# Turning some edge counts behind a layer's experts, making masks tile by tile, and starting a row product between the turns

## The chip, the cores and the metric

The kernel runs on one core of a Trainium2 chip. A core has a matrix engine (TensorE, PE in the profile, whose weight loads are listed as PEld), three engines for elementwise work (VectorE or DVE, ScalarE or ACT, GpSimd or POOL), queues that start transfers (SP among them) and 16 DMA engines. The metric is the device time of one execution in microseconds (us). Three runs of the kernel before took 1514.17 to 1518.64 us, with a median of 1517.61.

## The reference

The program is a chain of four layers on 625 nodes with 512 features and 10,000 directed edges. Each layer is a graph part and an expert part, and each part adds its result to x after a layer normalisation of its input:

```
edge_index = jnp.stack([src, dst])
x = x + _L0_gnn_ref(_layernorm(x, axis=-1), edge_index, ...)
x = x + _L0_ffn_ref(_layernorm(x, axis=-1)[None], ...)[0]
x = x + _L1_gnn_ref(_layernorm(x, axis=-1), edge_index, ...)
...
x = x + _L3_gnn_ref(_layernorm(x, axis=-1), edge_index, ...)
x = x + _L3_ffn_ref(_layernorm(x, axis=-1)[None], ...)[0]
```

Three of these parts meet the change. The expert part of layer L0 has eight small experts, each of which is computed for every node and weighted by a gate:

```
hid = jax.nn.gelu(jnp.einsum('bnd,edf->bnef', y, W1) + b1)
eo = jnp.einsum('bnef,efd->bned', hid, W2) + b2
out = jnp.einsum('bned,bne->bnd', eo, gate)
```

The graph part of layer L1 is an attention over the edges, twice. For each edge a score of its two ends is taken, the scores of a target's edges go through a softmax, and the values of the sources are summed with these weights:

```
scores = jnp.einsum('ehd,ehd->eh', q[tgt], k[srcidx])
m = jax.ops.segment_max(scores, tgt, num_segments=n)
p = jnp.exp(scores - m[tgt])
s = jax.ops.segment_sum(p, tgt, num_segments=n)
w = p / (s[tgt] + 1e-16)
agg = jax.ops.segment_sum(w[:, :, None] * v[srcidx], tgt, num_segments=n)
```

The graph part of layer L3 multiplies the rows by a matrix, sums them over the edges with a loop at each node, and normalises over the nodes:

```
xw = x @ W.T
...
msgs = norm[:, None] * xw[row]
out = jax.ops.segment_sum(msgs, col, num_segments=n)
```

## The kernel before

The 625 nodes lie in five tiles of 125 (`NT`, `T`), the 512 features in four blocks of 128 (`KD`). x stays on the chip with nodes on the partitions. Products need the features on the partitions, so each normalised tile is turned: `to_features` (L400) takes, per tile, four transposes on PE (L408) into one bank of PSUM and copies it out by `evac` (L267 on DVE, L275 on ACT, by turns). All uses of PSUM share one pool of four buffers that go round.

The edges are held as a matrix of counts, `aT`, source by target: the setup builds it by products of one-hot columns. The attention of L1 treats the graph as a dense matrix: for each target tile it computes all 625 scores, adds a mask of -1e30 where the count is zero (L1263), takes the exponential (L1268) and multiplies by the count (L1278). For this it needs the counts with targets on the partitions, `cnt`, and the mask of the same shape. `cnt` is made in front of the experts of L0: for each of five tiles, five transposes of blocks of `aT` (L1609) and two copies, one of 500 columns and one of 125. The mask is one instruction on POOL over all five tiles (L1618).

`small_experts` (L1201) runs the eight experts three ahead: `Hidden.half` (L1191) gives an expert's hidden units, `add` (L1211, L1213) its second product and the weighted sum into x on DVE. A bias of the experts is prepared by small copies on POOL and comes in by products (L634, L641). The last three experts go tile by tile, and behind each tile `ln.add` takes its statistics: for tiles 0 and 2 by two passes on ACT (L343, L344), for the others by DVE (L335, L350). The normalisation `LayerNorm` closes in two groups, tiles 0 to 2 and tiles 3 and 4: a square root on ACT (L296), some small steps on DVE (L300 to L309), and then the tiles themselves by turns on DVE (L371) and ACT (L377), the latter after `ln_nb` (L374). At its end `small_experts` issues two products whose result nobody reads (`warm`, L398).

In L1 the query projection goes through `mm_groups` (L466): it takes all four PSUM buffers at once and its results are copied by four instructions on DVE (L1669). The key projection (L477) and its copies follow, and then the first scores (L1257). Five additions of a bias row to x (L1688) are queued behind the last query copy.

In L3 the normalised rows are turned first, all five tiles, and then `mm_nodes` (L485) multiplies them tile by tile by the weights, with the results copied by DVE and ACT by turns (L1901); the product with `aT` follows (L477). The profile lists two passes for one such product of float32: a tile's row product of four steps is eight passes.

The order of instructions on each engine is not that of the source: a scheduler sets it when the program is built, from the data dependencies and the order of the source, and `tc.issue_after(i)` keeps what it encloses behind the instruction i on its engine. An example that matters here: the addition of the identity to the diagonal blocks of `aT` (named `loop` in `normalise`, L1646), written in the second half of L1, stands on DVE directly behind the count turns, since each waits only for the turn that reads its block. Weights come in chunks of 1 MB into three buffers, asked for by `take` on SP's queue.

Of the kernel before, what the change touches and what calls it, by code (L numbers as in the profile page):

```python
# [13 lines left out]
BF16 = mybir.dt.bfloat16  # L14
I32 = mybir.dt.int32
AF = mybir.ActivationFunctionType
OP = mybir.AluOpType
# [3 lines left out]
N = 625  # L21
NT = 5
T = N // NT
HC = 313
NP = 2 * HC
# [8 lines left out]
NEG = -1.0e30  # L34
# [161 lines left out]
def kernel(  # L196
# [11 lines left out]
    nc = tc.nc  # L208
# [20 lines left out]
    ident = const.tile([P, P], F32, name="ident")  # L229
# [82 lines left out]
    GROUPS = ((0, 3), (3, NT))  # L312
# [73 lines left out]
    def pstile(name):  # L386
        return psum.tile([P, 2, 512], F32, tag="ps", name=name)

    pe = {}

    def warm(n, behind=True):

        if n == 0:
            return
        with tc.issue_after(pe["last"].ins) if behind else nullcontext():
            ps = pstile("ps_warm")
            for _ in range(n):
                nc.tensor.matmul(ps[:, 0, :HC], ident, rows[:, :HC], start=True, stop=True)  # L398

    def to_features(src, name, scale=None, bias=None):  # L400

        dst = ttile(name)
        nc.gpsimd.memset(dst[:, :, N:NP], 0.0)
        if bias is None:
            for t in range(NT):
                ps = pstile("ps_tr")
                for k in range(KD):
                    pe["last"] = nc.tensor.transpose(ps[:, 0, k * T:(k + 1) * T],  # L408
                                                     src[:, t, k * P:(k + 1) * P], ident[:T, :T])
                evac(dst[:, :, t * T:(t + 1) * T],  # L410
                     ps[:, 0, :KD * T].rearrange("p (k t) -> p k t", t=T), scale)
        else:
            for k in range(KD):
                ps = pstile("ps_tr")
                for t in range(NT):
                    nc.tensor.transpose(ps[:, t // 4, (t % 4) * T:(t % 4 + 1) * T],
                                        src[:, t, k * P:(k + 1) * P], ident[:T, :T])
                s, b = scale[:, k:k + 1], bias[:, k:k + 1]
                evac(dst[:, k, :4 * T], ps[:, 0, :4 * T], s, b)
                evac(dst[:, k, 4 * T:N], ps[:, 1, :T], s, b)  # L420
        return dst
# [776 lines left out]
                if e == E - 1:  # L1198
                    table_of(AF.Sqrt, done)

    def small_experts(hidden, comb, layer, ln):  # L1201

        hs, ws = hidden.hs, hidden.ws

        def ahead(e):
            hidden.half(e, 0)
            hidden.half(e, 1)

        def add(e, t):
            ps = pstile("ps_eo")  # L1210
            pe["last"] = nc.tensor.matmul(ps[:T, 0, :], hs[e][:, t * T:(t + 1) * T],  # L1211
                                          ws[e // 4][1][:, e % 4, :], start=True, stop=True)
            nc.vector.scalar_tensor_tensor(x[:, t, :], ps[:T, 0, :], comb[:, t, e:e + 1],  # L1213
                                           x[:, t, :], op0=OP.mult, op1=OP.add)

        bias = expert_bias(comb, layer)
        bias.pop(0)()
        for e in range(len(hs), 3):
            ahead(e)
        for e in range(E - 3):  # L1220
            ahead(e + 3)
            for step in bias[3 * e - 3:3 * e] if e else ():
                step()
            for t in range(NT):
                add(e, t)

        for t in range(NT):
            for e in range(E - 3, E):
                add(e, t)
            ln.add(t, x[:, t, :], t in (0, 2))  # L1230
        warm(2)

    def attention(qT, kT, v, mask, counts, pt_pool, s_pool, values=lambda: None):

# [136 lines left out]
    aT = aT1[:T]  # L1371
    dg = const.tile([P, NP], F32, name="dg")
    xn = ktile("xn")
    hT = ttile("hT")
    with tc.tile_pool(name="setup", bufs=1) as setup, \
# [11 lines left out]
        for src in srcs:  # L1387
# [7 lines left out]
                                       op0=OP.mult, op1=OP.add)  # L1395
        nc.vector.tensor_scalar(digit[:, 1, :], digit[:, 0, :], float(BASE - 1), 1.0, op0=OP.mult,
                                op1=OP.add)
# [204 lines left out]
    with tc.tile_pool(name="l1g", bufs=1) as pool:  # L1602

        cnt = pool.tile([T, NT, NP], F32, name="cnt")
        nc.gpsimd.memset(cnt[:, :, N:NP], 0.0)
        for t in range(NT):
            ps = pstile("ps_ct")
            for j in range(NT):
                nc.tensor.transpose(ps[:T, j // 4, (j % 4) * T:(j % 4 + 1) * T],  # L1609
                                    aT[:, j, t * T:(t + 1) * T], ident[:T, :T])  # L1610
            evac(cnt[:, t, :4 * T], ps[:T, 0, :4 * T])
            evac(cnt[:, t, 4 * T:N], ps[:T, 1, :T])
        xn = ktile("xn")
        with tc.tile_pool(name="l0h", bufs=4) as hpool:
            small_experts(Hidden(yT, vec("L0_ffn_b1"), hpool), gate, 0,
                          LayerNorm(xn, groups=GROUPS))
        mask = pool.tile([T, NT, NP], BF16, name="mask")
        nc.gpsimd.tensor_scalar(mask, cnt, 0.0, NEG, op0=OP.is_equal, op1=OP.mult)  # L1618

# [32 lines left out]
        def step(n):  # L1654
            for work in steps[:n]:
                work()
            del steps[:n]

        xT = to_features(xn, "xT")
        for l in range(2):  # L1660
            if l == 1:
                normalise()
            with tc.tile_pool(name=f"l1p{l}", bufs=2) as pt_pool, \
                    tc.tile_pool(name=f"l1s{l}", bufs=4) as s_pool:
                (w,) = take(1)
                qT = ttile("qT")
                for o, ps in enumerate(mm_groups(
                        ONE, KD, lambda o, k: w[:, k, o * P:(o + 1) * P], xT)):
                    last = nc.vector.tensor_scalar(halves(qT[:, o, :]), ps,  # L1669
                                                   vec("L1_gnn_bq", l)[:, o:o + 1], DH ** -0.5,  # L1670
                                                   op0=OP.add, op1=OP.mult)
                    step(2)
                (w,) = take(1)
                kT = ttile("kT")
                for o in range(KD):
                    ps = mm_features([(w[:, k, o * P:(o + 1) * P], xT[:, k, :]) for k in range(KD)])
                    evac(halves(kT[:, o, :]), ps)
                    step(2)
                (w,) = take(1)
                v = ktile("v")  # L1680

                def values():
                    for t in range(NT):
                        evac(v[:, t, :], mm_nodes(xT, w, t))
                        step(2)
                        if l == 0:
                            with tc.issue_after(last.ins):
                                nc.vector.tensor_add(x[:, t, :], x[:, t, :], row("L1_gnn_ln_b"))  # L1688

                oT = attention(qT, kT, v, mask, cnt, pt_pool, s_pool, values)  # L1690
                assert not steps
            (w,) = take(1)
            hT = ttile("hT")
            bn = BatchNorm(hT, THREE, vec("L1_gnn_g1", l), vec("L1_gnn_beta1", l), AF.Identity)
            for o in range(KD):
                ps = mm_features([(w[:, k, o * P:(o + 1) * P], oT[:, k, :]) for k in range(KD)])
                with bn.behind():
                    nc.vector.scalar_tensor_tensor(halves(hT[:, o, :]), ps,
                                                   vec("L1_gnn_bo", l)[:, o:o + 1],
                                                   halves(xT[:, o, :]), op0=OP.add, op1=OP.add)  # L1700
                    bn.add(o)
            (w,) = take(1)
            wf = w.rearrange("p k m -> p (k m)")
            (ps,) = mm_groups(THREE, 1, lambda o, k: wf[:, k * P:(k + 1) * P], hT)
            f = pool.tile([P, NP], F32, name="f", tag="f")
            nc.scalar.activation(halves(f), ps, AF.Relu, bias=vec("L1_gnn_b1", l))
            xT = ttile("xT")
            bn = BatchNorm(xT, TWO if l else ONE, vec("L1_gnn_g2", l), vec("L1_gnn_beta2", l),
                           AF.Identity)
            for o in range(KD):  # L1710
                ps = mm_features([(wf[:, D + o * P:D + (o + 1) * P], f)])
                with bn.behind():
                    nc.vector.scalar_tensor_tensor(halves(xT[:, o, :]), ps,
                                                   vec("L1_gnn_b2", l)[:, o:o + 1],
                                                   halves(hT[:, o, :]), op0=OP.add, op1=OP.add)
                    bn.add(o)
            warm(2)
# [175 lines left out]
        small_experts(hidden, comb, 2, LayerNorm(xn, groups=GROUPS))  # L1893


    xnT = to_features(xn, "xnT")
    (w,) = take(1)
    xw = ktile("xw")
    for t in range(NT):
        ps = mm_nodes(xnT, w, t)  # L1900
        last = nc.scalar.copy(xw[:, t, :], ps) if t % 2 else nc.vector.tensor_copy(xw[:, t, :], ps)  # L1901
    with tc.issue_after(last.ins):
        for t in range(NT):
            nc.vector.tensor_add(x[:, t, :], x[:, t, :], xn[:, t, :])
# [54 lines left out]
```

## Time and profile before

| | before |
|---|---|
| median of three runs | 1517.61 us (1514.17 to 1518.64) |
| profiled execution | 1512.58 us, span 1510.9 us |
| PE busy | 1434.1 us, 95% |
| DVE, ACT, POOL busy | 664.5, 389.0, 200.2 us |
| mean granted clock of PE | 0.985 |
| instructions | 18457 |

A timeline line gives the start, the time from the first start to the last end, the engine, the source line, the operation with its output and input, the shape, and how many were merged; in brackets stands how long the engine was idle before, and whose end let it go on. The granted clock is the share of PE's full speed that was allowed in a stretch. All times of single places are from the profiled execution.

### The profile page before, as it was taken

The page shows a single profiled execution, that of the slowest core. Times are in us where ns is not written, and L with a number is a line of the kernel's source. Part 1 is how long each engine was busy: PE and PEld are TensorE (multiplying, and loading weights), DVE is VectorE, ACT ScalarE, POOL GpSimd, SP SyncE. Part 2 cuts the span into 40 slices and gives each one's busy share as a digit, 9 for nine tenths or more (in the row PEclk, how much of TensorE's full clock was granted, in tenths as well). Part 3 has the DMA queues.
Part 4 walks back from the last instruction along what each step waited for, and adds up shares of the span by engine and source line. Part 5 has one row for each costly group of instructions (what it writes and reads, how often), then busy time and mean ns, then how long its engine had stood idle before and what let it go on. Part 6 is the DMA issues. An engine that isn't in the chain of part 4 may idle for free. (4 is left out here: it accounts for less than half of the span.)

```text
span 1510.9 us, 18457 instructions
## 1 busy us (share of the span) xinstructions
PE 1434.1 (95%) x7048; PEld 1002.9 (66%) x7048; DVE 664.5 (44%) x1793; ACT 389.0 (26%) x768; POOL 200.2 (13%) x344
## 2 busy tenths in 40 slices
PE   9999999999999999997999998999989999999996
PEld 6775466656565665565665886554667669999885
DVE  9945463363876546847512125746361101111100
ACT  2133273211466124633101105412130000001000
POOL 1010041300143013310202210000001001101000
PEclk9999999999999999998999999999999999999998
DMA  4010100111100110001768523000059326457880
GB/s 153 6 43 29 56 28 5 52 56 56 56 1 1 56 56 0 1 1 34 317 229 324 157 60 131 28 28 28 0 183 402 141 81 201 163 183 265 312 290 5
DMA packets 28915, 159.39 MB, mean 105 GB/s; under 512 B 3952, under 2 KB 4080, under 8 KB 11921
## 3 DMA queue, kind: packets, MB, share of 16 engines
q1 hardware_dynamic: 20791, 141.56, 25.5%
q0 software_dynamic: 5280, 11.27, 3.5%
q10 hardware_dynamic: 2746, 5.25, 1.1%
q8 instruction: 60, 0.98, 0.3%
q14 instruction: 38, 0.31, 0.1%
HBM read 166.49 MB, written 11.31 MB: 118 GB/s over the span
## 5 line engine op out<-in xcount | busy, mean ns | idle before, releaser
L955 PE MATMUL ps_h<-xgT,ring 128*128 128x128 f32 (+5 forms) x1920 | 318.6, 326 | 0.1
L955 PEld LDWEIGHTS ps_h<-xgT,ring 128*128 128x128 f32 x1920 | 276.5, 191 | 38.9 <-issue 3.5
L1286 POOL TENSOR_SCALAR s<-s,rs 125x625 f32<-125x625 f32 (+4 forms) x120 | 96.3, 820 | 307.5 <-DVE rs L1283 284.8
L1045 PE MATMUL ps_y<-hT,ring 128*128 128x352 f32 (+4 forms) x640 | 137.0, 373 | 0.0
L1045 PEld LDWEIGHTS ps_y<-hT,ring 128*128 128x128 f32 x640 | 108.7, 190 | 24.3 <-issue 0.2
L1925 DVE TENSOR_TENSOR hT<-ps_h,g 128x512 f32<-128x512 f32 (+4 forms) x60 | 27.8, 464 | 198.5 <-ACT g L1924 192.1
L1268 ACT ACTIVATE s<-s,mn 125x626 f32<-125x626 f32 (+4 forms) x120 | 87.2, 743 | 61.0 <-DVE mn L1263 61.0
L1263 DVE CUSTOM_DVE_ANT_0 s<-ps_s,mask 125x626 f32<-125x626 f32 (+4 forms) x120 | 82.2, 718 | 30.9 <-PE ps_s L1257 29.9
L1924 ACT ACTIVATE g<-ps_h 128x512 f32<-128x512 f32 (+4 forms) x60 | 25.0, 416 | 250.8 <-PE ps_h L955 250.8
L1257 PE MATMUL ps_s<-kT,qT 64*125 64x313 f32 (+4 forms) x416 | 84.3, 454 | 5.1 <-DVE mn L1263 5.1
L915 POOL DMA_INDIRECT slots<-rows_hbm,node x26 | 25.5, 981 | 357.0 <-PE ps_x L933 190.3
L1278 DVE SCALAR_TENSOR_TENSOR s<-s,cnt 125x626 f32<-125x626 f32 x80 | 66.4, 849 | 12.2 <-ACT s L1268 12.1
L1300 PEld LDWEIGHTS ps_p<-ident,s 125*125 125x125 f32 x432 | 52.4, 190 | 28.6 <-issue 15.0
L1211 PE MATMUL ps_eo<-w,h 128*125 128x512 f32 x160 | 70.5, 593 | 0.6 <-ACT h L1196 0.6
L1321 PE MATMUL ps_o<-pT,v 125*64 125x375 f32 (+2 forms) x448 | 60.1, 413 | 9.1 <-DVE mn L1263 4.6
L1300 PE MATMUL ps_p<-ident,s 125*125 125x125 f32 x432 | 63.2, 288 | 4.2 <-DVE mn L1263 1.7
L1257 PEld LDWEIGHTS ps_s<-kT,qT 64*125 64x125 f32 x416 | 43.7, 184 | 32.3 <-DVE mn L1263 12.0
L1078 PE MATMUL ps_y<-ring,hT 128*128 128x512 f32 x128 | 56.9, 593 | 0.0
L1424 PE MATMUL ps_a<-dst,src 125*128 125x313 f16 x400 | 55.0, 297 | 1.3 <-DVE dst L1410 0.9
L1211 PEld LDWEIGHTS ps_eo<-w,h 128*125 128x125 f32 x160 | 29.8, 187 | 36.4 <-issue 30.7
L485 PE MATMUL ps_mn<-w,hxT 128*125 128x512 f32 x120 | 52.0, 593 | 0.6 <-ACT hxT L277 0.6
L267 DVE COPY yT<-ps_y 128x352 f32<-128x352 f32 (+4 forms) x17 | 7.2, 425 | 102.4 <-PE ps_y L1045 102.4
(424 smaller groups left out, 2016.1 us busy)
## 6 DMA issues: line engine op xcount, KB each, us to landing
ring<-in_weights SPq DMA_DIRECT2D x122, 1024.0 KB
w<-in_weights SPq DMA_DIRECT2D x27, 1024.0 KB
rows_hbm<-xn ACTq DMA_DIRECT2D x2, 1120.0 KB
x<-in_x SPq DMA_DIRECT2D x1, 1120.0 KB
sums<-x ACTq DMA_DIRECT2D x1, 1120.0 KB
x<-sums SPq DMA_DIRECT2D x5, 224.0 KB
out<-x ACTq DMA_DIRECT2D x1, 1120.0 KB
rows<-in_rows SPq DMA_DIRECT2D x1, 1052.0 KB
```

The lines of the kernel that those rows point to most:

```text
L955: pe["last"] = nc.tensor.matmul(ps[:, m, g * n:(g + 1) * n], w[:, k, j * P:(j + 1) * P], xgT[:, k, :n], start=(k == 0), stop=(k == KD - 1))
L1045: nc.tensor.matmul(ps[:, 0, :n], second(i, f)[:, d * P:(d + 1) * P], hT[:, f, :n], start=(f == 0), stop=(f == nf - 1))
L1078: nc.tensor.matmul(ps[:, 0, :], hT[:, f, m * B:m * B + rows], second(i, f), start=(f == 0), stop=(f == nf - 1))
L1211: pe["last"] = nc.tensor.matmul(ps[:T, 0, :], hs[e][:, t * T:(t + 1) * T], ws[e // 4][1][:, e % 4, :], start=True, stop=True)
L1257: nc.tensor.matmul(ps[hh][:T, i, :w], qT[rr, b, t * T:(t + 1) * T], kT[rr, b, i * w:(i + 1) * w], start=True, stop=True)
L1263: nc.vector.tensor_tensor_reduce(s[:, hh, :nb * w].rearrange("p (a c) -> p a c", a=nb), ps[hh][:T, :nb, :w], mask[:, t, :nb * w].rearrange ...
L1268: nc.scalar.activation(s[:, hh, :nb * w], s[:, hh, :nb * w], AF.Exp, bias=mn[:, hh:hh + 1], scale=-1.0, accum_out=sm[:, hh:hh + 1] if caus ...
L1278: nc.vector.scalar_tensor_tensor(s[:, hh, :], s[:, hh, :], 1.0, counts[:, t, :], op0=OP.mult, op1=OP.mult, accum_out=sm[:, hh:hh + 1])
L1286: nc.gpsimd.tensor_scalar(s[:, hh, :w], s[:, hh, :w], rs[:, hh:hh + 1], 1.0, op0=OP.mult, op1=OP.mult)
L1300: nc.tensor.transpose(pp[:T, hh, j * T:(j + 1) * T], s[:, hh, j * T:(j + 1) * T], ident[:T, :T])
L1321: nc.tensor.matmul(po[rr, 0, o:n * T], v[:, j, h * DH:(h + 1) * DH], pT[:, hh, j, o:n * T], start=(j == 0), stop=(j == nk - 1))
L1424: nc.tensor.matmul(pa[b // 2][:, b % 2, :HC], srcs[c % SRCS][:, b, :], dsts[c][:, :HC], start=(c == c0), stop=(c == c1 - 1))
```

## The change

The turning of the counts is put into a function of the tile, `turned`. Tiles 0 and 1 are turned where all five were, and each of these two is masked on POOL right away. Tiles 2 to 4 are turned by `others`, which `small_experts` calls in place of its two warm products, with all copies on ACT. Their masks are made on DVE, each behind one of the last three query copies of L1's first attention. In L3, `to_features` calls a function between the turns of tile 2 and tile 3, and this does the first tile's row product.

```diff
-    def to_features(src, name, scale=None, bias=None):
+    def to_features(src, name, scale=None, bias=None, between=None):
...
             for t in range(NT):
+                if t == 3 and between is not None:
+                    between(dst)
                 ps = pstile("ps_tr")
...
-    def small_experts(hidden, comb, layer, ln):
+    def small_experts(hidden, comb, layer, ln, fill=lambda: warm(2)):
...
-        warm(2)
+        fill()
...
-        for t in range(NT):
+        mask = pool.tile([T, NT, NP], BF16, name="mask")
+
+        def turned(t, copies):
             ps = pstile("ps_ct")
             for j in range(NT):
-                nc.tensor.transpose(ps[:T, j // 4, (j % 4) * T:(j % 4 + 1) * T],
-                                    aT[:, j, t * T:(t + 1) * T], ident[:T, :T])
-            evac(cnt[:, t, :4 * T], ps[:T, 0, :4 * T])
-            evac(cnt[:, t, 4 * T:N], ps[:T, 1, :T])
+                pe["last"] = nc.tensor.transpose(ps[:T, j // 4, (j % 4) * T:(j % 4 + 1) * T],
+                                                 aT[:, j, t * T:(t + 1) * T], ident[:T, :T])
+            copies[0](cnt[:, t, :4 * T], ps[:T, 0, :4 * T])
+            copies[1](cnt[:, t, 4 * T:N], ps[:T, 1, :T])
+
+        def masked(engine, t):
+            engine.tensor_scalar(mask[:, t, :], cnt[:, t, :], 0.0, NEG, op0=OP.is_equal,
+                                 op1=OP.mult)
+
+        def others():
+
+            for t in range(2, NT):
+                with tc.issue_after(pe["last"].ins):
+                    turned(t, (nc.scalar.copy, nc.scalar.copy))
+
+        for t in range(2):
+            turned(t, (evac, evac))
+            masked(nc.gpsimd, t)
         xn = ktile("xn")
         with tc.tile_pool(name="l0h", bufs=4) as hpool:
             small_experts(Hidden(yT, vec("L0_ffn_b1"), hpool), gate, 0,
-                          LayerNorm(xn, groups=GROUPS))
-        mask = pool.tile([T, NT, NP], BF16, name="mask")
-        nc.gpsimd.tensor_scalar(mask, cnt, 0.0, NEG, op0=OP.is_equal, op1=OP.mult)
+                          LayerNorm(xn, groups=GROUPS), others)
...
                                                    op0=OP.add, op1=OP.mult)
+                    if l == 0 and o > 0:
+                        with tc.issue_after(last.ins):
+                            masked(nc.vector, o + 1)
                     step(2)
...
-    xnT = to_features(xn, "xnT")
     (w,) = take(1)
     xw = ktile("xw")
-    for t in range(NT):
+
+    def weighted_rows(xnT, t):
         ps = mm_nodes(xnT, w, t)
-        last = nc.scalar.copy(xw[:, t, :], ps) if t % 2 else nc.vector.tensor_copy(xw[:, t, :], ps)
+        return nc.scalar.copy(xw[:, t, :], ps) if t % 2 else nc.vector.tensor_copy(xw[:, t, :], ps)
+
+    xnT = to_features(xn, "xnT", between=lambda dst: weighted_rows(dst, 0))
+    for t in range(1, NT):
+        last = weighted_rows(xnT, t)
```

## The prediction

> **What bounds the kernel now.** I read the busy shares first, then the chain that ended last, then the two places that the change touches as timelines, last the granted clock of their stretches.
>
> ```profile
> PE 1434.1 (95%) x7048; PEld 1002.9 (66%) x7048; DVE 664.5 (44%) x1793; ACT 389.0 (26%) x768; POOL 200.2 (13%) x344
> ...
> PE 34%; issue 2%; DVE 2%; ACT 1%; DMA 1%; POOL 0%; ACTq 0%; POOLq 0%; DVEq 0%
> ```
>
> TensorE (PE) is busy 95% of the span and leads the chain. So a pass taken off PE's unbroken stretches shortens the run; one put into a hole of PE costs nothing.
>
> The first place, layer L0's experts. PE before them:
>
> ```profile
> 266.98 2.56 PE L1609 MATMUL ps_ct<-ident,aT 125*125 125x125 f32 x22
> 269.38 17.03 PE L1191 MATMUL ps_mf<-yT,w 128*128 128x313 f32 x64
> ```
>
> The count turns stand directly ahead of the experts with no hole between them: 2.56/22 = 0.116 us each on the path. Behind the experts, where x is normalised and turned:
>
> ```profile
> 340.68 1.22 PE L398 MATMUL ps_warm<-rows,ident 128*128 128x313 f32 x4
> ...
> 342.94 0.65 PE L408 MATMUL ps_tr<-ident,xn 125*128 125x125 f32 x4 [1.04 <-DVE xn L371]
> 342.99 0.81 ACT L377 ACTIVATE xn<-x,ln_nb,ln_r 125x512 f32<-125x512 f32 x1 [4.07 <-DVE ln_nb L374]
> ...
> 346.52 0.65 PE L408 MATMUL ps_tr<-ident,xn 125*128 125x125 f32 x4 [1.59 <-DVE xn L371]
> ```
>
> PE waits here 1.04 us for the first normalised tile and 1.59 us for the second group (tiles 3, 4). ACT has been idle 4.07 us before its tile.
>
> The second place, the start of layer L3, has the same shape, and then its row products:
>
> ```profile
> 1047.48 0.65 PE L408 MATMUL ps_tr<-ident,xn 125*128 125x125 f32 x4 [1.05 <-DVE xn L371]
> 1048.40 1.07 PE L408 MATMUL ps_tr<-ident,xn 125*128 125x125 f32 x8 [0.27 <-ACT xn L377]
> 1051.49 2.01 PE L408 MATMUL ps_tr<-ident,xn 125*128 125x125 f32 x8 [2.02 <-DVE xn L371]
> 1053.30 19.38 PE L485 MATMUL ps_mn<-w,xnT 128*125 128x512 f32 x40
> ```
>
> The hole is 2.02 us, and the 40 passes behind it take 19.38 us. Why so long, the clock column tells (stretch, length, busy time of PE, PEld, DVE, ACT, POOL, clock, DMA share, GB/s):
>
> ```profile
> 1049.50:1051.50 2.00, 0.01 (x1) 0.01 (x1) 1.85 (x7) 0.35 (x2) 0.00 (x0) 0.77 0.00 0
> 1051.50:1053.30 1.80, 1.80 (x9) 1.59 (x10) 0.00 (x1) 1.39 (x2) 0.00 (x0) 0.50 0.00 0
> 1053.30:1057.30 4.00, 4.00 (x6) 1.65 (x6) 0.68 (x1) 0.00 (x0) 0.00 (x0) 0.50 0.01 4
> 1057.30:1064.00 6.70, 6.70 (x17) 2.89 (x16) 0.69 (x1) 0.59 (x1) 0.00 (x0) 0.99 0.00 0
> ```
>
> 0.77 over 2 us means half clock from about 1050.6; it lasts to about 1057.4, 6.8 us. Weight loads of these passes stand 0.428 us apart at full clock, 0.855 us at half.
>
> **The change, part by part.** All against the profiled execution: 1512.58 us, span 1510.9.
>
> (a) Fifteen of the 25 count turns leave the stretch before the experts: 15 x 0.116 = -1.75 us. The built order of PE puts the experts' first product straight behind the ten that stay. Its chunk was asked for long before, and DMA is at 0 while it runs, so no load takes the place of the turns. Three of the five additions of the identity to aT (L1646) move away with their turns.
>
> (b) The fifteen turns stand where two warm products stood, behind the last expert. Four passes of 1.22 us go, 15 x 0.116 = 1.75 us come, from 340.7 to 342.4 on the old time axis. The next turn waits for its tile until 342.94, so PE pays nothing. What may pay is the normalisation. ACT now copies six pieces of PSUM in its idle 4.07 us: the 500-wide ones follow each other at 0.45 to 0.56 us, the 125-wide take 0.27. From 341.4 that is ct2 to 342.1, ct3 to 342.8, the wide part of ct4 to 343.2; then comes tile 1's normalisation (before 342.99): +0.2 us, and +0.65 if each copy costs its full duration (3 x 0.56 + 2 x 0.28 from 341.4). The sixth copy stands before the first xT copy and the second group's square root on ACT: +0.3 there. On VectorE (DVE) three additions of 0.28 us stand in the second group's chain; two fall into its waits, and that chain has waited for ACT and the turns at 344.5 anyhow. I take +0.25 for the second group, from 0 to +0.85 (all three additions in full).
>
> (c) The masks. On POOL one instruction of 10.84 us (five tiles, 2.17 each) becomes two of a tile each, 4.3 us, ahead of the expert bias's pieces, which ended at 272.9 and would end near 277; PE takes them at 294.76: hidden by 18 us. If POOL were far slower than that, PE would wait at L634. Three tiles are masked on DVE between the qT copies. No such row exists; the nearest is L371, 125x512 in 0.54 us, so 0.66 for 626 columns; the far end is POOL's 2.17. The qT copies have 1.24 us of idle between them. The third mask stands before five additions (3.09 us) and the first kT copy, which moves from 370.87 by 0.3 to 2 us; PE needs that bank again and kT itself at 383.41. Nothing on the path. The first scores wait for masks that are 10 us old.
>
> (d) L3's first row product (8 passes) goes ahead of the turns of tiles 3 and 4. It needs xnT's tile 0 (copied by 1049.13), its weights (chunk landed by about 1030) and a bank that only the warm products used. So it starts at 1049.5, when the third turn ends, and at full clock lasts 8 x 0.428 = 3.42 us, to 1052.9. The turns, ready at 1051.44 and 1052.35, now wait for it: 1052.9 to 1053.9. The remaining 32 passes take 13.7 us, to 1067.6; before, the next stage (L477) began at 1072.51. That is -4.9 us: 2.0 the hole, about 0.85 the two slow turns with the gap between them, 2.1 the half clock after 1053.3. DVE copies the product's result behind ln_nb, so the normalisation waits for nothing new; DVE's copy of tile 4 is queued behind it, at about 1054, and its reader comes only as the fifth product.
>
> The clock part rests on rows. It fell after a 3.4-us stretch with 1.7 us of PE work (1047.2 to 1050.6) and did not fall after 340.6 to 344.0 with some 2.1 us. With the product in the hole the emptiest such stretch holds 1.31 us idle, 2.1 busy. Bounds of (d): -1.5, if the clock falls all the same at 1050.6 for 6.8 us (the passes then lose 3.4 us of the 4.9); -5.4, if all holes close and the fall of before would on average have been 0.5 us dearer. I take -4.9, nearer to the row with 2.1 busy.
>
> [...]
>
> (e) At the first place the half clock ran from 347.4 to 350.9 and cost 1.3 us of the q product. Here one low stretch, L3 two: nothing in the rows fixes the number, so another execution may have two here too, until 354.2, and lose half of 5.9, 2.9 us. Against this profile I add the middle, +0.8.
>
> Sum: -1.75 + 0.25 + 0 - 4.9 + 0.8 = -5.6 us. The profiled execution is 5.0 us below the median of 1517.61, and the three runs spread over 4.5 us, so I carry the difference over: 1517.61 - 5.6 = 1512.0. A tenth of a per cent is 1.5 us; 0.3%, 4.55 us, is about what a measurement of this kernel can tell from no change.
>
> **The rivals.** *The clock falls all the same in L3.* For it: all twelve turns before the product are short and sparse. Against: 2.1 us busy held the clock once. (d) becomes -1.5, the sum -2.2: 1515.4.
>
> *The hand-over to layer L1 gives its part back.* For it: ACT and DVE get nine instructions in a chain that PE waits for. Against: ACT's 4.07 us idle. Price: +0.85 in place of +0.25 and two low stretches, +1.6 in place of +0.8: the sum is -4.2, 1513.4.
>
> *Slower: the product blocks the turns at half clock.* If the clock falls before 1049.5 and stays, the product takes 6.85 us and everything behind it runs double: product to 1056.3, turns of 0.65 each to 1057.7, 32 passes of 0.855 to 1085, 12.5 us later than before; with (a), (b) and (e) 1517.61 + 12.5 - 0.7 = 1529.4. It decides from some 11 us of half clock on, where it has eaten (d)'s 4.9 and the 0.7. Against: at both places the clock came back after 3.4 to 6.8 us of work.
>
> That the change does not do what it says is excluded by the built order: the turns, masks and product stand where described, and no other instruction or load changes place.
>
> **How the numbers follow.** Main case 0.68; clock rival 0.12; hand-over rival 0.13; slower 0.07. Of the main case 0.13 is put within 0.3%, since 5.6 is only 1 us past the bound and medians move by more; both small rivals are within it. Faster 0.55, same 0.38, slower 0.07. The range goes down to 1508.0 (all of (d)'s -5.4, no (e), -6.9, and 2.7 us of scatter) and up to 1516.5 (the clock rival with 1 us of scatter).
>
> **What the profile after would show.** L1191 begins about 1.75 us earlier; the start of the second group's turns (L408, before at 346.52) stays within 0.3 us of its place relative to the last expert; masks at L1620 on DVE of about 0.66 us. In L3 the hole of 2.02 us is filled by 8 passes, the clock stays 1.00 through the row products, and from the first turn to L477 it takes 20.1 us in place of 25.0. The prediction is wrong if the clock there reads 0.5 for over 3 us, or if tile 1's normalisation moves by more than 0.65 us.

## The result

The changed kernel took 1511.59 us (median of 9 runs, 1509.07 to 1513.78), the kernel before, beside it, 1515.91 (9 runs, 1514.17 to 1518.64). The ratio is 0.9966, with a 95% interval of 0.9955 to 0.9978: faster by 0.2 to 0.5%. In two further comparisons it came out at 0.9962 [0.9948, 0.9976] and 0.9960 [0.9944, 0.9975].

The profiled execution after took 1511.75 us, 0.8 us less than the profiled execution before; its span, 1509.9 us, is 1.0 us shorter. So the two profiles must not be subtracted as wholes. They are read stretch by stretch, and the places of the change are much as forecast. In front of the experts of L0 (timeline of PE after; the first line is the start of the gate logits, the second the last seven of the ten turns that stayed):

```profile
264.30 1.71 PE L566 MATMUL ps_lg<-yT,lg_w 128*64 128x313 f32 x8
...
268.81 0.93 PE L1614 MATMUL ps_ct<-ident,aT 125*125 125x125 f32 x7
269.57 17.03 PE L1194 MATMUL ps_mf<-yT,w 128*128 128x313 f32 x64
```

The experts still begin directly behind the turns, which now take 0.93 us in place of 2.56. From the first gate logits to the experts it is 5.27 us (264.30 to 269.57) after 6.91 (262.47 to 269.38): -1.64. Behind the experts (all engines; the last PE line, the start of the key product, is counted only up to the edge of the view):

```profile
340.87 1.80 PE L1614 MATMUL ps_ct<-ident,aT 125*125 125x125 f32 x15
341.62 0.58 ACT L1616 COPY cnt<-ps_ct 125x500 f32<-125x500 f32 x1 [2.50 <-PE ps_ct L1614]
...
343.22 0.62 PE L411 MATMUL ps_tr<-ident,xn 125*128 125x125 f32 x4 [0.55 <-DVE ln_nb L374]
343.33 0.86 ACT L377 ACTIVATE xn<-x,ln_nb,ln_r 125x512 f32<-125x512 f32 x1
...
347.00 1.92 PE L411 MATMUL ps_tr<-ident,xn 125*128 125x125 f32 x8 [1.68 <-DVE ln_nb L374]
348.71 19.13 PE L469 MATMUL ps_mg<-xT,w 128*128 128x313 f32 x64
...
364.45 0.48 DVE L1620 TENSOR_SCALAR mask<-cnt 125x626 bf16<-125x626 f32 x1
...
367.68 4.64 PE L480 MATMUL ps_mf<-xT,w 128*128 128x313 f32 x17
```

The fifteen turns stand in the hole, and the wait for the first tile is 0.55 us in place of 1.04. ACT's tile no longer has idle time before it: the copies reach up to it. The second group's turns come 3.78 us behind the first in place of 3.58. The query product takes longer than before (18.97 us until the key product in place of 18.14), and the clock says why. First the windows of the kernel before, then of the one after:

```profile
344.00:347.00 3.00, 1.41 (x12) 1.11 (x11) 2.22 (x10) 1.57 (x4) 0.00 (x0) 1.00 0.31 128
347.00:350.00 3.00, 2.73 (x10) 2.01 (x9) 0.68 (x1) 0.96 (x2) 0.00 (x0) 0.57 0.00 0
350.00:353.00 3.00, 3.00 (x11) 2.09 (x10) 0.00 (x0) 0.00 (x0) 0.00 (x0) 0.86 0.00 0
```

```profile
344.00:347.00 3.00, 1.08 (x9) 0.88 (x9) 2.78 (x13) 1.64 (x6) 0.00 (x0) 0.85 0.38 158
347.00:350.00 3.00, 3.00 (x11) 2.48 (x12) 0.68 (x1) 1.35 (x2) 0.00 (x0) 0.50 0.00 0
350.00:353.00 3.00, 3.00 (x7) 1.89 (x7) 0.00 (x0) 0.00 (x0) 0.00 (x0) 0.51 0.00 0
```

Half clock for 3.4 us before, for 6.8 us after. At the start of L3 it is the other way round (timeline of PE, then windows, of after):

```profile
1052.40 1.07 PE L411 MATMUL ps_tr<-ident,xn 125*128 125x125 f32 x8 [0.27 <-ACT xn L377]
1053.31 3.60 PE L488 MATMUL ps_mn<-w,xnT 128*125 128x512 f32 x8
1056.75 1.02 PE L411 MATMUL ps_tr<-ident,xn 125*128 125x125 f32 x8
1057.61 13.90 PE L488 MATMUL ps_mn<-w,xnT 128*125 128x512 f32 x32
1071.34 21.24 PE L480 MATMUL ps_mf<-aT,xw 125*128 125x313 f32 x80
```

```profile
1053.00:1057.00 4.00, 4.00 (x16) 2.02 (x15) 2.30 (x11) 1.58 (x3) 0.00 (x0) 1.00 0.00 0
1057.00:1061.00 4.00, 4.00 (x16) 2.11 (x15) 1.32 (x2) 0.58 (x1) 0.00 (x0) 1.00 0.01 4
```

No hole, no half clock: from the first turn to the product with aT 19.85 us (1051.49 to 1071.34) in place of 25.03. With the query projection counted from the first turn of its tiles to the start of the key product, the changed places sum to -1.64 + 0.09 (experts to first turn) + 0.94 (24.46 in place of 23.52) - 5.18 = -5.8 us. The rest of the profile, in which no edit moves work of PE, gave 4.8 us back; the experiments show where.

### The profile page after: what moved, and what is told of

Same layout as the page of the kernel before. It is cut to its first block, busy times and chain, and to the rows that moved or that the text cites. A ratio compares the mean times of both kernels' runs of the same rounds, so it can differ in the third digit from the quotient of the medians.

```text
span 1509.9 us, 18457 instructions
## 1 busy us (share of the span) xinstructions
PE 1435.1 (95%) x7044; PEld 1004.1 (67%) x7044; DVE 665.3 (44%) x1793; ACT 389.4 (26%) x771; POOL 194.1 (13%) x345
## 5 line engine op out<-in xcount | busy, mean ns | idle before, releaser
L1214 PEld LDWEIGHTS ps_eo<-w,h 128*125 128x125 f32 x160 | 29.9, 188 | 36.4 <-issue 30.7
```

## The experiments

Each run is compared with the kernel before on the same chip. From each one's profile I read the same four stretches (us): *logits*, first gate logits to experts; *hand-over*, first turn to the end of L1's query product; *between*, from there to L3's first turn; *L3*, first turn to the product with aT. Of the change only the last mask on DVE reaches into *between*, and PE does not wait for it: the first scores start 16.95 us behind the key product in the profiles before and after alike. The last column is the time at half clock inside *between*, from the trace's record of the granted clock.

| kernel | logits | hand-over | between | L3 | half clock between |
|---|---|---|---|---|---|
| before | 6.91 | 23.52 | 681.0 | 25.03 | 20.5 |
| changed | 5.27 | 24.46 | 683.8 | 19.85 | 27.3 |
| changed, second | 5.28 | 24.40 | 681.9 | 19.85 | 20.5 |
| changed, third | 5.28 | 23.64 | 682.9 | 19.85 | 23.9 |
| row alone | 6.91 | 23.39 | 684.7 | 19.85 | 30.7 |
| counts alone | 5.28 | 23.65 | 684.0 | 24.02 | 27.3 |
| warm in hole | 6.92 | 23.55 | 683.1 | 22.57 | 23.9 |
| two rows | 5.28 | 23.66 | 683.8 | 19.86 | 27.3 |
| turns in hole | 5.28 | 22.03 | 685.7 | 19.85 | 30.7 |
| query in hole | 5.27 | 20.58 | 681.7 | 19.85 | 23.9 |
| query in hole, second | 5.28 | 20.58 | 684.4 | 19.86 | 27.3 |

**The two halves of the change.** `row_alone` is the kernel before with the L3 edit, `counts_alone` the changed kernel with L3 as before:

```diff
 row_alone
...
-    xnT = to_features(xn, "xnT")
...
+    xnT = to_features(xn, "xnT", between=lambda dst: weighted_rows(dst, 0))
...
 counts_alone
...
-    xnT = to_features(xn, "xnT", between=lambda dst: weighted_rows(dst, 0))
...
+    xnT = to_features(xn, "xnT")
...
```

> Only part (d): L3's first row product between the turns of tiles 2 and 3; the counts stay as before. Theory (hole and clock): -4.9 us in the profile's own L3 stretch (first turn to the product with aT 25.0 -> 20.1 us), clock 1.00 there; on the median -3.5 to -5 us of the kernel before. Rival (the clock falls all the same): the stretch shortens by 1.5 to 2.9 us, clock 0.5 for over 3 us in it, median -1.5 to -3.

> Only parts (a) to (c): counts of three tiles turned behind L0's experts, masks by tiles; L3 as before. Theory: -1.7 us in front of the experts, +0.1 to +0.4 behind them, so -1.3 to -1.6 on the median, and L3's hole of 2.0 us and its half clock are there as before. Rival (the hand-over gives it back): the median within 0.5 us of the kernel before.

Measured: `row_alone` 1511.60 us (8 runs) against 1516.62, ratio 0.9963 [0.9947, 0.9978]; `counts_alone` 1514.41 (11 runs), 0.9982 [0.9971, 0.9994]. The stretches are as expected, the medians at the far edge (-5.0) and past it (-2.2 where -1.3 to -1.6 was expected, though the interval, -0.9 to -4.4 us, holds that). In the profile of `counts_alone` L3 is 1.0 us shorter than in the profile before, since the clock was low for a shorter time; that is no work of the edit. So the row product makes most of the gain and the counts a smaller gain that is clear of zero; the hand-over does not give it all back. In `counts_alone` the hole of L3 is there (timeline of PE), and the clock fell, for 3.4 us this time:

```profile
1054.50 0.70 PE L411 MATMUL ps_tr<-ident,xn 125*128 125x125 f32 x4 [2.02 <-DVE xn L371]
1055.42 1.09 PE L411 MATMUL ps_tr<-ident,xn 125*128 125x125 f32 x4 [0.22 <-ACT xn L377]
1056.31 18.36 PE L488 MATMUL ps_mn<-w,xnT 128*125 128x512 f32 x40
```

**The clock by itself.** `warm_in_hole` moves nothing; it puts four products that nobody reads into L3's hole of the kernel before:

```diff
...
-    xnT = to_features(xn, "xnT")
+    xnT = to_features(xn, "xnT", between=lambda dst: warm(4))
```

> The kernel before with four products whose result nobody reads (8 passes of 0.26 us, 2.1 us) in L3's hole, nothing moved: this adds work and fills the hole for the clock alone. Theory (the clock falls because a 3.4-us stretch is too empty): the clock stays 1.00, the 40 passes take 17.1 to 17.3 us in place of 19.4, first turn to the product with aT 22.2 to 22.6 us in place of 25.0, median -2 to -3 us. Rival (the fall has another cause): 25.0 us or more, median 0 to +0.3 us.

Measured: 1514.92 us (12 runs) against 1516.62, ratio 0.9988 [0.9977, 0.9999]: by the medians -1.7 us, short of the 2 to 3 us expected and only just clear of zero. The profile is as expected. Timeline of PE, and a window:

```profile
1053.36 2.28 PE L398 MATMUL ps_warm<-rows,ident 128*128 128x313 f32 x8
1055.64 0.62 PE L410 MATMUL ps_tr<-ident,xn 125*128 125x125 f32 x4
1056.46 0.65 PE L410 MATMUL ps_tr<-ident,xn 125*128 125x125 f32 x4 [0.21 <-ACT xn L377]
1056.94 17.33 PE L487 MATMUL ps_mn<-w,xnT 128*125 128x512 f32 x40
```

```profile
1056.00:1060.00 4.00, 3.79 (x15) 1.86 (x14) 0.68 (x1) 0.87 (x2) 0.00 (x0) 1.00 0.01 4
```

With 2.28 us of work added, the stretch is 2.46 us shorter than in the profile before and 1.45 shorter than in `counts_alone`: the 40 passes take 17.33 us at full clock. All profiles together agree: in L3 the clock fell in the two with the hole open and in none of the nine with something in it; in the hand-over to L1 it fell in all eight with the hole open and in none of the three with something in it. So the fall hangs on the empty stretch.

How empty it must be, the record of the clock shows for these two places. The low stretches last one or more steps of 3.413 us, so the time can be divided into windows along these steps. All ten falls at the two places come behind a window with 1.40 to 1.78 us of PE work; no window there with 2.09 us or more is followed by one. Where the first low window held 2.41 to 2.52 us of PE work, a second low window followed (three falls); where it held 3.15 us or more, none did (seven). This is no rule for the whole kernel: at other places windows with 1.42 to 2.03 us were followed by no fall and one with 2.18 us was, so the busy time alone does not decide.

The Trainium skill, "TensorE: Matmul & The Clock Gate", section "HAM oscillation", gives as its abstract rule that PE should have no idle gap above about 3.4 us. Here the clock fell around a gap of 2.02 us behind twelve sparse turns, so the trace goes beyond that rule.

The change's 5.18 us in L3, taken against the profile before, divide into 2.46 for the clock and 2.72 (22.57 to 19.85) for real work in the hole; against `counts_alone`, whose clock was low for half as long, the clock's part is 1.45.

**Does it hurt that the turns wait?** `two_rows` puts two row products ahead, so the turns wait another 3.4 us:

```diff
-    xnT = to_features(xn, "xnT", between=lambda dst: weighted_rows(dst, 0))
-    for t in range(1, NT):
+    xnT = to_features(xn, "xnT", between=lambda dst: (weighted_rows(dst, 0), weighted_rows(dst, 1)))
+    for t in range(2, NT):
```

> The changed kernel with two row products in place of one ahead of the turns of tiles 3 and 4, so the turns wait another 3.4 us. Theory (PE is never idle there, the order of its work is free): first turn to the product with aT 19.9 us as in the changed kernel, time within 0.5 us of it. Rival (late turns cost, since their copies and the last products stand behind them): up to +3.4 us.

> The changed kernel once more, as the mark for the three runs beside it: -3.5 to -5 us of the kernel before.

Measured side by side: `two_rows` 1510.04 us (8 runs), 0.9951 [0.9934, 0.9967]; the changed kernel 1509.86 (11 runs), 0.9962 [0.9948, 0.9976]; L3 takes 19.86 and 19.85 us. The turns' delay costs nothing, since PE is never idle there.

**The other hole.** The hand-over to L1 still has its hole of 1.68 us and its half clock. Two ways to fill it: `turns_in_hole` moves the fifteen count turns there (and the two warm products back behind the experts), `q_in_hole` starts the query product there.

```diff
 turns_in_hole
...
-        xT = to_features(xn, "xT")
+        xT = to_features(xn, "xT", between=lambda dst: others())
 q_in_hole
...
+        def first_half(dst):
+            q0.append(pstile("ps_mg"))
+            for k in range(KD):
+                pe["last"] = nc.tensor.matmul(q0[0][:, 0, :HC], wq[:, k, :P], dst[:, k, :HC],
+                                              start=(k == 0), stop=(k == KD - 1))
...
-        xT = to_features(xn, "xT")
+        xT = to_features(xn, "xT", between=first_half)
...
```

In `q_in_hole` the rest of the product follows block by block in a PSUM buffer each, since the first form takes all four at once.

> The changed kernel with the fifteen count turns not behind the last expert but between the turns of tiles 2 and 3 of the hand-over, and the two warm products back. Theory (turns fill the hole for PE, their six copies on ACT then stand ahead of tile 4's normalisation and of xT's copies): PE pays nothing for the turns, ACT delays tile 4 by some 1 us; the clock is what decides: if turns count as work it stays 1.00 and the time is within 1 us of the changed kernel or up to 1 us below; if they do not, +1 us.

> The changed kernel, and in the hand-over to L1 the first half of the first block of the query product (8 passes, 2.1 us) between the turns of tiles 2 and 3, the query product then block by block. Theory (hole and clock, as in L3): the hole of 1.68 us is filled, the clock stays 1.00 from 344 to 356, which cost 2.1 us in the changed kernel's profile; the product needs tile 2's copy, so the turns of tile 3 come up to 1 us later: in sum -1 us for the moved passes and -1 to -2 for the clock, so 2 to 3 us below the changed kernel. Rival (the clock falls there for the sparse turns all the same): -1 us.

> The kernel with the query half product in the hand-over once more, for its distance to the changed kernel. Theory from the first profile (hand-over and query product 20.6 us in place of 23.7 to 24.4): median 3 to 4 us below the changed kernel beside it, 0.993 to 0.995 of the kernel before. Rival (the first six runs were lucky): within 1.5 us of the changed kernel.

> The changed kernel beside it: 0.9955 to 0.9978 of the kernel before, as in its first nine runs; L3 from the first turn to the product with aT 19.9 us, hand-over and query product 23.6 to 24.5 us.

Measured: `turns_in_hole` 1509.66 us (10 runs), 0.9953 [0.9938, 0.9967]; `q_in_hole` 1506.37 (6 runs), 0.9939 [0.9918, 0.9961], with the changed kernel at 1509.86 beside both. The second time, `q_again` 1505.77 (5 runs), 0.9929 [0.9912, 0.9945], and the changed kernel 1510.47 (8 runs), 0.9960 [0.9944, 0.9975]. So this version beats both kernels: it is 3.5 and 4.7 us below the changed one, each time a little more than expected (2 to 3 and 3 to 4). Its hand-over (timeline of PE, and a window) has a wait of 0.67 us where there was one of 1.68, and the clock held in both its profiles:

```profile
345.39 2.37 PE L1682 MATMUL ps_mg<-xT,w 128*128 128x313 f32 x8 [0.67 <-ACT xT L275]
347.60 1.02 PE L411 MATMUL ps_tr<-ident,xn 125*128 125x125 f32 x8
348.45 14.92 PE L1690 MATMUL ps_mg<-xT,w 128*128 128x313 f32 x56
```

```profile
350.00:353.00 3.00, 3.00 (x13) 2.14 (x12) 0.87 (x1) 0.00 (x0) 0.00 (x0) 1.00 0.00 0
```

In the one profile of `turns_in_hole` the clock held too, and the hand-over is 22.03 us, 1.6 to 2.4 less than in the changed kernel; its median does not show that, and the same profile has the longest *between* of all, 685.7 us. Whether turns hold the clock in every execution stays open.

**Where the profile's other 4.8 us went.** In *between*, the length of the eleven profiles grows with the time at half clock: 20.5 us of it go with 681.0 and 681.9; 23.9 with 681.7 to 683.1; 27.3 with 683.8 to 684.4; 30.7 with 684.7 and 685.7. The profile of the changed kernel had 6.8 us more of it than the profile before and was 2.8 us longer there. Another 1.8 us of the difference lies ahead of the first logits, which came between 262.4 and 264.4 us in all these profiles; its cause stays open. The remaining 0.2 lies behind L3. The runs of each kernel scatter in the same way, by 2.5 to 8.1 us.

## Why the prediction was right

The time forecast, 1512.0 us, is 0.4 off, in part by good luck: the step that carried the sum to the median of three runs used 1517.61, and more runs put the kernel before at 1515.91. From there the sum of -5.6 gives 1510.3; measured were -4.3 us by the medians and -3.3 to -6.8 by the ratio's interval. By the ratios of the three comparisons it was -5.2, -5.8 and -6.1 us, so the sum itself was good.

By its steps:

- (a) was -1.64 where -1.75 was forecast.
- (b) was forecast as +0.25 for the second group and came as +0.29 against the experts' start: +0.09 for the first turn and +0.20 more behind it. Tile 1's normalisation on ACT moved by 0.15 us, well inside the 0.65 named as a sign of being wrong.
- (c) Nothing reached the path, and the first kT copy did not move (4.42 us behind the start of the key product after 4.41), but both prices were off: the mask on DVE took 0.478 us, less than the 0.66 that I had scaled up from 0.54 of a row with fewer columns, and POOL 2.33 us each in place of 2.17; the experts' bias pieces ended at 278.4, with 16 us to spare.
- (d) was -5.18 against -4.9. `warm_in_hole` shows both its parts, though they divide otherwise: 2.72 us for work in the hole and 2.46 for the clock, where I had 2.0 for the hole and some 2.95 for the slow turns and the clock. Against `counts_alone`, in which the clock had fallen for one stretch alone, it was -4.2.
- (e) The second stretch of half clock came, and that it cost +0.83 us, as much as the +0.8 put in as a middle, is luck. A second stretch was priced at +1.6; it cost half of that, since the low time began at 346.1, while PE still waited, so that 4.2 us of the query product fell into it after 2.5 before. In the third profile of the changed kernel it did not come, and the hand-over took 23.64 us, 0.1 more than before. I had written that nothing in the rows fixes the number of stretches; the ten falls above show that at these two places it goes with where the windows of 3.413 us stand to the hole.

The rivals: the clock did not fall at the filled hole of L3 in any of the nine profiles that have something there. The hand-over gives back 0.1 to 0.9 us of its 1.6, not all. The product did not block the turns, not even at double length. Had the clock fallen all the same in L3, (d) would have been -1.5 us; it was -5.18.

## What to carry to other kernels

Where a chain of short steps leaves the matrix engine a hole, start the next product on the tiles that are ready: it fills the hole and keeps the clock up behind it, which here was worth about as much again (2.5 of 5.2 us, or 1.5 of 4.2 against the shorter fall). Cheap work moved from an unbroken stretch into a wait is gained where it leaves (1.64 us here); part of it can go again where it arrives (0.1 to 0.9 us here, the larger figure where the clock was low for longer), even though the engine that empties its results had idle time there. Compare profiles by stretches: two executions of one kernel can differ by as much as a change of this size brings.

## What had not been expected of the hardware

The same mask instruction (125x626, float32 in, bf16 out) takes 0.478 us on DVE and 2.33 us on POOL, 4.9 times as long; and DVE's 0.478 is less than the 0.54 us of its 125x512 instruction with float32 out. The falls of the clock begin, within one execution, whole multiples of 3.413 us apart: in the first profile of the changed kernel at 127.6, 346.1, 410.9 and 690.8 us, distances of 64, 19 and 82 of them, each fall up to L3 lasting one to three. The Trainium skill, "TensorE: Matmul & The Clock Gate", section "Part 1: The HAM clock gate", describes a free-running window of 3413 ns by which the clock is set, and the trace agrees. So one hole costs differently in executions of one and the same kernel: the hand-over took 23.6 to 24.5 us.
